# Layer 2's projections given out in denser steps and layer 1's in wider ones, in a list of sixteen interleaved graphs

## The chip, the cores and the metric

The kernel runs on one core of one Trainium2 chip. Its time is the device time of one execution in microseconds, the median over several executions. All executions told of here are in the fast state, so that no difference below mixes states. "The profile" is one execution taken by the hardware profiler. Its engines are PE (TensorE matrix products), PEld (TensorE weight loads), DVE (VectorE), ACT (ScalarE), POOL (GpSimd) and SP (SyncE); a q behind an engine's name marks its queue of issued transfers.

## The reference

Sixteen graphs of 1024 nodes with 256 features pass through four layers. Each layer normalizes, applies a ReLU, computes a graph layer and adds the result to its input.

```python
for layer in (L0, L1, L2, L3):
    h = jnp.maximum(_layernorm(x, axis=-1), 0.0)
    x = x + layer(h, adj)
# L0: h W, attention with a softmax over columns, elu
# L1: h W, attention with a softmax over rows, elu
# L2: relu(h W_upd + mean of the neighbours' h W_msg + bias)
# L3: attention with 4 heads of 64, relu, a norm of its own per head
```

All arithmetic is in float32. The sixteen graphs do not depend on each other.

## The kernel before

Each graph is a Python generator that emits instructions and yields a number: how many list units later its next piece is to stand. One loop merges all graphs into one list. Graph b starts at 120 b, and a graph's yields add up to some 260 units, so its second half stands beside the first half of the next graph.

```python
APART = 120.0
queue = [(33, 0, more())] + [(b * APART, b, graph(b)) for b in range(B)] + [(b * APART - 60, b, loads(b)) for b in range(1, B)]
while queue:
    queue.sort(key=lambda g: g[:2])
    at, b, g = queue.pop(0)
    ...
        queue.append((at + next(g), b, g))
```

A scheduler then makes a fixed order for each engine out of this list; it may move instructions past others, except where `later` keeps instructions in program order. At run time each engine works through its order; in the traces below an engine stands before an instruction that waits although other work is listed behind it.

```python
def graph(b):
    ...
    for g in range(NT // 2):                 # NT = 8
        norm.pair(xs, g)                     # L623: statistics of x on DVE
        m.step()
        yield 2
    for layer, inputs in ((layer0, (m,)), (layer1, (m.bytes,)), (layer2, ())):
        yield 2
        ...
        yield from layer(b, xs, *inputs, norm, after)
    yield 2
    ...                                      # layer 3, then the tail (L929 to L946)
```

Layer 0 has eight projections, then a row that goes to memory and comes back on all partitions, then eight weight tiles on DVE. Two output tiles are accumulated while the weights are made, the "early pairs":

```python
def layer0(b, xs, m, norm, after):
    for n in range(NT):
        ps = project(norm, wx[0], n, D + 2)          # L659 on PE; PSUM pool of 2 buffers
        nc.scalar.activation(hs[:, n, : D + 2], ...) # L717
        m.step()
        yield 1.2
    row_a, row_b = [everywhere(d, "row") for d in spread(column(...), 1, (1.0, S), "l0")]
    ...            # spread: PE L672 transposes the column, SP L678 writes it; everywhere: SP L684 reads the row
    yield 5
    for j in range(NT):
        nc.vector.scalar_tensor_tensor(p, row_a, q[:, j : j + 1], row_b, ...)        # L740
        nc.vector.scalar_tensor_tensor(p, p, 1.0, mask[:, j, :], ...)                # L742
        nc.scalar.activation(hs[:, j, :D], hs[:, j, :D], AF.Copy, scale=z[:, 1:2])   # L744
        ...        # early pair j - 1: PE L730, held in program order by later
        yield 2.6
    ...            # the eighth early pair, then six more output tiles, yield 3.9 each
```

The two loops that change, and what follows them:

```python
def layer1(b, xs, mask, norm, after):
    for n in range(NT):
        ps = project(norm, wx[1], n, D + 2)
        nc.scalar.activation(hs[:, n, : D + 2], ps[:, : D + 2], AF.Copy, scale=norm.rs[n])   # L773
        yield 1.2
    ...
    yield 5
    ...            # eight weight tiles on DVE (L793), yield 1.3 each; eight outputs on PE (L786), 3.9 each

def layer2(b, xs, norm, after):
    ...
    for n in range(NT):
        ps = project(norm, wx[2], n, 2 * D)
        nc.scalar.activation(hi[:, n, :D], ps[:, :D], ...)      # L832
        nc.scalar.activation(rest, ps[:, :D], ...)              # L834
        nc.scalar.activation(up[:, n, :D], ps[:, D:], ...)      # L835
        nc.vector.tensor_tensor(lo[:, n, :D], ...)              # L836
        nc.vector.tensor_tensor(up[:, n, :D], ...)              # L837
        yield 1.9
    for j in range(NT):
        ...        # one message tile: 16 products (PE L844) on the adjacency (POOL L585), ACT L853 empties it
        yield 3.5
```

Layer 3 waits 8 units after its projections, then makes 4 heads of 8 weight tiles (DVE L887, PE L893). The tail is DVE work of 128x1024 (L941 to L945) and ends with the output stores on SyncE (L946). The input of graph b is loaded by GpSimd (L545) into one of three buffers, so this load waits for the last L945 of graph b - 3, which read that buffer.

Of the kernel before, what the change touches and what calls it, by code (L numbers as in the profile page):

```python
# [421 lines left out]
def tile_simple_stack(  # L422
# [233 lines left out]
    def project(norm, w, n, width):  # L656
        ps = mm_ps.tile([P, HALF], F32, tag="mm", name="ps_proj")
        for c in range(DC):
            nc.tensor.matmul(ps[:, :width], norm.ht[:, c, n * P : (n + 1) * P], w[:, c, :width], start=(c == 0), stop=(c == DC - 1))  # L659
        return ps  # L660

    def new_hs(name="hs"):
        return state.tile([P, NT, W3], F32, tag="hs", name=name, bufs=4)

    def spread(col, n, scales, name):




        k = n * NT  # L670
        ps = tr_ps.tile([P, P], F32, tag="tr", name="ps_col")
        nc.tensor.transpose(ps[:k, :], col, ident)  # L672
        all_rows = []
        for scale in scales:
            e = small.tile([H * NT, P], F32, tag="e_row", name="e_row", bufs=2)
            nc.scalar.activation(e[:k, :], ps[:k, :], AF.Exp, scale=scale)
            d = dram.tile([n, N], F32, tag=f"row_{name}", name="d_row", bufs=4)
            later(nc.sync.dma_start(d.rearrange("r (t p) -> (r t) p", p=P), e[:k, :]))  # L678
            all_rows += [d[r] for r in range(n)]
        return all_rows  # L680
# [6 lines left out]
    def column(src, n):  # L687

        col = small.tile([P, H, NT], F32, tag="col", name="col", bufs=2)
        nc.vector.tensor_copy(col[:, :n, :], src.rearrange("p t n -> p n t"))  # L690
        return col[:, :n, :].rearrange("p n t -> p (n t)")
# [5 lines left out]
    def weights(name):  # L697
        return work.tile([P, N], F32, tag="p", name=name, bufs=NT)
# [70 lines left out]
    def layer1(b, xs, mask, norm, after):  # L769
        hs = new_hs()  # L770
        for n in range(NT):
            ps = project(norm, wx[1], n, D + 2)
            nc.scalar.activation(hs[:, n, : D + 2], ps[:, : D + 2], AF.Copy, scale=norm.rs[n])  # L773
            yield 1.2
        (d_row,) = spread(column(hs[:, :, D + 1 : D + 2], 1), 1, (S - 1.0,), "l1")
        row = everywhere(d_row, "row")
        watch(b, 1, hs[:, :, D : D + 2])
        q = small.tile([P, NT], F32, tag="q", name="q")
        nc.scalar.activation(q, hs[:, :, D], AF.Exp, scale=1.0 - S)
        nc.scalar.activation(hs[:, :, D], hs[:, :, D], AF.Exp, scale=S)  # L780
        yield 5
        ps_ = []
        early = [at_ps.tile([P, HALF], F32, tag="at", name="ps_o1") for _ in range(EARLY)]

        def product(ps, i, j):
            nc.tensor.matmul(  # L786
                ps[:, : D + 1], ps_[j][:, i * P : (i + 1) * P], hs[:, j, : D + 1], start=(j == 0), stop=(j == NT - 1)
            )

        for j in range(NT):  # L790
            nc.scalar.activation(hs[:, j, :D], hs[:, j, :D], AF.Copy, scale=hs[:, j, D : D + 1])
            p = weights("p1")
            nc.vector.scalar_tensor_tensor(p, row, q[:, j : j + 1], mask[:, j, :], op0=OP.max, op1=OP.mult)  # L793
            ps_.append(p)
            for i, ps in enumerate(early):
                product(ps, i, j)
            yield 1.3
        for i in range(NT):
            if i < EARLY:
                ps = early[i]  # L800
            else:
                ps = at_ps.tile([P, HALF], F32, tag="at", name="ps_o1")
                for j in range(NT):
                    product(ps, i, j)
            k = b * NT + i
            z = shares[:, k : k + 1]
            nc.vector.reciprocal(z, ps[:, D : D + 1])  # L807
            e = work.tile([P, D], F32, tag="e", name="e")
            nc.scalar.activation(e, ps[:, :D], AF.Exp, scale=z)  # L809
            v = work.tile([P, D], F32, tag="v", name="v")  # L810
            nc.scalar.activation(v, ps[:, :D], AF.Copy, scale=z)
            residual(xs, i, v, after, e)
            yield 3.9


    def layer2(b, xs, norm, after):
# [12 lines left out]
        for n in range(NT):  # L829
            ps = project(norm, wx[2], n, 2 * D)  # L830
            rs = norm.rs[n]
            nc.scalar.activation(hi[:, n, :D], ps[:, :D], AF.Copy, scale=rs)  # L832
            rest = work.tile([P, D], F32, tag="e", name="rest")
            nc.scalar.activation(rest, ps[:, :D], AF.Copy, scale=rs)  # L834
            nc.scalar.activation(up[:, n, :D], ps[:, D:], AF.Copy, scale=rs)  # L835
            nc.vector.tensor_tensor(lo[:, n, :D], rest, hi[:, n, :D].bitcast(F32), op=OP.subtract)  # L836
            nc.vector.tensor_tensor(up[:, n, :D], up[:, n, :D], rows["bias2"], op=OP.add)  # L837
            yield 1.9
        for j in range(NT):
            g, jj = divmod(j * P, QUART)  # L840
            ps = hd_ps.tile([P, HALF], F32, tag="hd", name="ps_o2")
# [240 lines left out]
```

## Time and profile before

| | |
|---|---|
| time | 2778.73 us (2765.97 to 2779.11) |
| span of the profiled execution | 2770.2 us |
| from the column transpose (L672) of layer 0 in one graph to that in the next, mean of graphs 3 to 14 | 166.8 us |
| start to the transpose of graph 1; transpose of graph 15 to the end | 158.5 us; 278.9 us |

The prediction shows the lines that bound the kernel. In a line of the page, behind the first bar stand the busy time and the mean ns of one instruction, behind the second the idle time ahead of the group and what ended most of it. Three lines of the view of waits are needed later: the waiting engine, tile and line, what it waited for, then microseconds in total, times, and the longest.

```profile
PE ps_o L730 <- ACT hs L744: 50.0, 29, 13.3
...
PE ps_proj L659 <- ACT up L835: 6.9, 17, 2.1
...
PE ps_o L786 <- DVE p L793: 3.7, 10, 0.4
```

Only the first is large: it is layer 0's early pairs, standing at the head of PE's order and waiting for the weights.

### The profile page before, as it was taken

How to read it: one execution, taken by the hardware profiler on the slowest of the kernel's cores; microseconds unless marked ns; L12 is line 12 of the kernel's file. 1: busy time of each engine (PE TensorE's matmuls, PEld its weight loads, DVE VectorE, ACT ScalarE, POOL GpSimd, SP SyncE). 2: the span in 40 equal slices, each digit the busy share in tenths (PEclk: the TensorE clock that was granted, in tenths of full speed). 3: DMA queues.
4: the chain of work that ended last, by engine and by line, in shares of the span. 5: the costliest groups of instructions: out<-in, count | busy, mean ns of one | idle time of the engine just before them, and what ended most of it. 6: DMA issues, size and time to landing. Idle time of an engine off the chain costs nothing.

```text
span 2770.2 us, 62256 instructions
## 1 busy us (share of the span) xinstructions
PE 2540.6 (92%) x25682; PEld 2014.7 (73%) x25682; DVE 2024.4 (73%) x4069; ACT 1440.6 (52%) x4065; POOL 371.8 (13%) x390
## 2 busy tenths in 40 slices
PE   5899999999999999999999999999999999999975
PEld 4677777777777767777776777767787677777754
DVE  4357768687676877768787676977768787676868
ACT  4563654627466373654627466373654637555250
POOL 1000110202011020210202111011210202111011
PEclk8899999999999999999999999999999999999997
DMA  4421322414124142322414124142332414223121
GB/s 150 105 77 55 110 72 68 114 52 137 51 74 118 60 118 67 97 76 78 115 52 137 52 78 114 59 119 66 96 77 78 115 51 126 62 66 95 40 62 34
DMA packets 146071, 233.71 MB, mean 84 GB/s; under 512 B 9392, under 2 KB 94512, under 8 KB 145776
## 3 DMA queue, kind: packets, MB, share of 16 engines
q1 hardware_dynamic: 74608, 145.73, 16.7%
q0 software_dynamic: 71168, 83.89, 12.0%
q8 instruction: 204, 3.34, 0.5%
q14 instruction: 91, 0.75, 0.1%
HBM read 212.35 MB, written 17.24 MB: 83 GB/s over the span
## 4 chain that ended last, share of the span: by engine, by line
PE 39%; DVE 22%; ACT 20%; issue 9%; DMA 7%; POOL 2%; SPq 0%; DVEq 0%; ACTq 0%; POOLq 0%
PE ps_o L893 11%; PE ps_o L730 9%; PE ps_proj L659 7%; PE ps_o L786 6%; DVE p L887 6%; ACT hn L631 5%; ACT unread L635 4%; DVE p L793 4%; DMA adj<-in_adj 3%; PE ps_o L844 3%; ACT mask L575 3%; DMA raw<-in_adj_t 2%; ACT ht L654 2%; PE pt_h L653 2%; DVE xs L708 1%
## 5 line engine op out<-in xcount | busy, mean ns | idle before, releaser
L887 DVE SCALAR_TENSOR_TENSOR p<-row,q,mask 128x1024 f32<-128x1024 f32 x512 | 636.8, 1280 | 62.3 <-DMA row<-d_row 41.3
L659 PE MATMUL ps_proj<-wx,ht 128*128 128x258 f32 (+2 forms) x2048 | 628.0, 444 | 21.4 <-ACT hs L717 9.9
L893 PEld LDWEIGHTS ps_o<-hb,p 128*64 128x64 f32 x16384 | 515.7, 138 | 157.3 <-issue 95.1
L893 PE MATMUL ps_o<-hb,p 128*64 128x65 f32 x16384 | 569.9, 225 | 43.1 <-DVE p L887 22.0
L730 PE MATMUL ps_o<-hs,p 128*128 128x256 f32 x2048 | 500.4, 388 | 56.1 <-ACT hs L744 50.0
L786 PE MATMUL ps_o<-hs,p 128*128 128x257 f32 x2048 | 526.8, 394 | 16.1 <-ACT mask L575 7.3
L659 PEld LDWEIGHTS ps_proj<-wx,ht 128*128 128x128 f32 x2048 | 364.8, 190 | 202.9 <-issue 72.3
L730 PEld LDWEIGHTS ps_o<-hs,p 128*128 128x128 f32 x2048 | 381.0, 193 | 118.2 <-ACT hs L744 59.8
L786 PEld LDWEIGHTS ps_o<-hs,p 128*128 128x128 f32 x2048 | 364.6, 190 | 79.6 <-issue 25.4
L707 DVE SCALAR_TENSOR_TENSOR xs<-e,xs 128x256 f32<-128x256 f32 x256 | 108.8, 425 | 323.5 <-ACT e L762 245.7
L631 ACT ACTIVATE hn<-xs,shift 128x256 f32<-128x256 f32 x512 | 237.5, 505 | 172.6 <-DVE shift L627 165.1
L809 ACT ACTIVATE e<-ps_o,shares 128x256 f32<-128x256 f32 x128 | 60.2, 470 | 422.1 <-DVE shares L807 422.0
L592 POOL TENSOR_SCALAR rs<-mv 128x4 f32<-128x4 f32 (+1 forms) x112 | 29.7, 265 | 1704.6 <-ACT unread L635 1694.1
L593 POOL TENSOR_TENSOR rs<-rs,neg_half 128x4 f32<-128x4 f32 (+2 forms) x144 | 238.3, 1665 | 8.2
L844 PE MATMUL ps_o<-hi,adj 128*128 128x258 f32 x1024 | 184.4, 313 | 25.3 <-DMA adj<-in_adj 15.6
L575 ACT ACTIVATE mask<-raw 128x512 uint8<-128x512 int32 x256 | 160.3, 630 | 66.1 <-DMA raw<-in_adj_t 65.3
L635 ACT ACTIVATE unread<-xs,shift 128x256 bf16<-128x256 f32 x384 | 193.1, 503 | 1.6
L653 PE MATMUL pt_h<-ident,hn 128*128 128x128 f32 x1024 | 174.2, 284 | 19.4 <-ACT hn L631 19.1
L654 ACT COPY ht<-pt_h 128x512 f32<-128x512 f32 x256 | 147.4, 588 | 72.2 <-PE pt_h L653 72.2
L653 PEld LDWEIGHTS pt_h<-ident,hn 128*128 128x128 f32 x1024 | 118.0, 142 | 84.6 <-ACT hn L631 63.3
L708 DVE SCALAR_TENSOR_TENSOR xs<-v,xs 128x256 f32<-128x256 f32 x384 | 161.8, 424 | 22.0 <-ACT v L764 3.5
L844 PEld LDWEIGHTS ps_o<-hi,adj 128*128 128x128 f32 x1024 | 143.5, 195 | 45.3 <-issue 15.8
(101 smaller groups left out, 2693.1 us busy)
## 6 DMA issues: line engine op xcount, KB each, us to landing
raw<-in_adj_t SPq DMA_DIRECT2D x256, 256.0 KB
adj<-in_adj POOLq DMA_DIRECT2D x64, 1024.0 KB, 5.9
row<-d_row SPq DMA_DIRECT2D x112, 512.0 KB
xs<-in_x POOLq DMA_DIRECT2D x32, 512.0 KB, 7.0
out<-res SPq DMA_DIRECT2D x32, 512.0 KB
wx<-in_w SPq DMA_DIRECT2D x3, 256.0 KB
d_row<-e_row SPq DMA_DIRECT2D x48, 4.0 KB
wts<-in_w_t SPq DMA_DIRECT2D x2, 256.0 KB
```

Of the source, the lines that this page charges most:

```text
L575: nc.scalar.activation(self.bytes[:, n, g * HALF : (g + 1) * HALF], raw, AF.Square, accum_out=squares[:, k : k + 1])
L593: nc.gpsimd.tensor_tensor(rs[:, :n], rs[:, :n], neg_half[:, :n], op=OP.pow)
L631: nc.scalar.activation(hn, xs[:, 2 * g + k, :], AF.Relu, bias=shift[:, k : k + 1])
L635: nc.scalar.activation(unread, xs[:, 2 * g + k, :], AF.Square, bias=shift[:, k : k + 1], accum_out=self.var[:, 2 * g + k : 2 * g + k + 1])
L653: nc.tensor.transpose(pt[:, c, k * P : (k + 1) * P], hn[:, c * P : (c + 1) * P], ident)
L654: nc.scalar.copy(self.ht[:, :, g * 2 * P : (g + 1) * 2 * P], pt)
L659: nc.tensor.matmul(ps[:, :width], norm.ht[:, c, n * P : (n + 1) * P], w[:, c, :width], start=(c == 0), stop=(c == DC - 1))
L730: m = nc.tensor.matmul(ps[:, :D], ps_[j][:, i * P : (i + 1) * P], hs[:, j, :D], start=(j == 0), stop=(j == NT - 1))
L786: nc.tensor.matmul(ps[:, : D + 1], ps_[j][:, i * P : (i + 1) * P], hs[:, j, : D + 1], start=(j == 0), stop=(j == NT - 1))
L844: nc.tensor.matmul(ps[:, : D + 2], adj_n[g][:, i, jj : jj + P], h[:, i, : D + 2], start=(h is hi and i == 0), stop=(h is lo and i == NT - 1),)
L887: nc.vector.scalar_tensor_tensor(p, row, q[:, j, h : h + 1], mask[:, j, :], op0=OP.max, op1=OP.mult)
L893: nc.tensor.matmul(pss[g][part, k * HW : (k + 1) * HW], p[:, i * P : (i + 1) * P][:, part], hbv[:, j, h, :], start=(j == 0 and k == 0), st ...
```

## The change

The intent is to move layer 2 against the next graph's layer 0. No instruction is added or removed, and two numbers change:

```diff
@@ layer1, behind each of its eight projections
-            yield 1.2
+            yield 1.4
@@ layer2, behind each of its eight projections
-            yield 1.9
+            yield 1.1
```

The places follow by adding up the yields. With the graph's start as 0, the next graph's layer 0 projects from 130.0 to 138.4 and makes weights from 144.6 on; its eighth early pair is listed at 165.4. Layer 2's first projection moves from 136.8 to 138.4, its first message from 152.0 to 147.2, layer 3's first projection from 182.0 to 177.2.

> **What bounds the kernel now.** I read the page first, then four windows that make one period of the steady state, then the order of work inside the first of them.
>
> ```profile
> span 2770.2 us, 62256 instructions
> PE 2540.6 (92%) x25682; PEld 2014.7 (73%) x25682; DVE 2024.4 (73%) x4069; ACT 1440.6 (52%) x4065; POOL 371.8 (13%) x390
> ...
> PE   5899999999999999999999999999999999999975
> ...
> PEclk8899999999999999999999999999999999999997
> ```
>
> The TensorE is the bound nearly everywhere. Only the first slice and the last two are thin, and neither end holds the two lines that change beside another graph for long. The clock is full after the first 140 us, so no clock effect is at stake. Sixteen graphs pass through, each starting 120 list units after the one before. From the first VectorE instruction of layer 0's weights (L740) of graph 6 (999.3) to that of graph 7 (1165.8) it is 166.5 us, and this repeats within a microsecond for all graphs from the third on. One such period, cut at the last layer-0 projection product of graph 6 (990.3), at its last early product (1027.0), at graph 5's first and last layer-3 product, and at the same projection point of graph 7:
>
> ```profile
> 990.30:1027.00 36.70, 31.74 (x165) 23.84 (x163) 34.03 (x71) 19.65 (x55) 5.80 (x8) 1.00 0.69 180
> 1027.00:1067.30 40.30, 39.54 (x201) 32.59 (x201) 17.88 (x54) 27.19 (x84) 6.42 (x8) 1.00 0.21 54
> 1067.30:1130.30 63.00, 60.51 (x1131) 49.55 (x1131) 56.52 (x92) 18.54 (x50) 3.83 (x5) 1.00 0.15 48
> 1130.30:1156.80 26.50, 25.15 (x111) 18.16 (x111) 17.53 (x38) 23.91 (x66) 7.00 (x6) 1.00 0.30 100
> ```
>
> The columns are PE, PEld, DVE, ACT and POOL busy. The first window is the one with most open PE time, 5.0 of 36.7 us, and there DVE is busy for 34.0: layer 0's weights make the pace. In that window layer 2 of graph 5 (projections, then messages) runs beside layer 0 of graph 6. Its end shows the mechanism:
>
> ```profile
> 1021.70 1.03 PE L730 MATMUL ps_o<-hs,p 128*128 128x256 f32 x4
> 1022.57 1.50 PE L659 MATMUL ps_proj<-wx,ht 128*128 128x264 f32 x6
> 1023.90 1.03 PE L730 MATMUL ps_o<-hs,p 128*128 128x256 f32 x4
> 1024.77 0.60 PE L653 MATMUL pt_h<-ident,hn 128*128 128x128 f32 x4
> 1026.94 1.13 PE L730 MATMUL ps_o<-hs,p 128*128 128x256 f32 x4 [1.57 <-ACT hs L744]
> ```
>
> PE stands still before the eighth early pair of layer 0, although two of layer 2's eight message tiles are still to do; they stand behind it in PE's order. Over the whole run that wait is one of the largest of PE:
>
> ```profile
> L730 PE MATMUL ps_o<-hs,p 128*128 128x256 f32 x2048 | 500.4, 388 | 56.1 <-ACT hs L744 50.0
> ```
>
> **What the Trainium skill says.** "Perfetto Trace Analysis", section Optimization Strategy, says that where the most contended engine changes over time, interleaving the regimes may help: this change moves such an interleaving. "TensorE: Matmul & The Clock Gate", section "Architectural detail", says that ACT and DVE queues are strictly in order and that TensorE can only pull weight loads ahead. The lines above agree: four transposes end at 1025.4 and nothing passes the pair that waits. Perfetto Trace Analysis, section Identifying the Most-Contended Engine, warns that matmul busy time is no measure of the distance to the limit. The trace agrees: if each matmul is given only the median step from one end to the next of its kind (0.436 us for a 258-column projection of two records, 0.858 for a 512-column one, 0.432 for layer 0's product, 0.434 for layer 1's, 0.120 for a message product, 0.067 for a layer-3 product, 0.110 for a transpose), a graph needs 147.3 us, so 19 of the 166.5 are lost, though PE shows 157 busy.
>
> **The change part by part.** No instruction is added or removed; both programs have the same counts. Only the list positions move: layer 2's eight projections take 8 x 1.1 = 8.8 units in place of 15.2, layer 1's 8 x 1.4 = 11.2 in place of 9.6. So layer 2's messages come 4.8 units earlier against the next graph, and layer 3 and the tail too. The scheduler turns list order into a fixed order per engine; I built the changed kernel and read that order for middle graphs, pricing PE rows with the steps above and DVE rows likewise (1.18 to 1.22 us for the 128x1024 ones, 0.34 to 0.43 for the 128x256 ones).
>
> Window 1, layer 0's column transpose to the eighth early pair. Before, the order has 30.4 us of PE work ahead of that pair and it took 36.5, a loss of 6.1. In the changed order all eight message tiles stand ahead of it: 33.0 us of work (34.1 for the later graphs). The chain that the pair waits for is hardly longer: DVE from the first L740 to the last L742 has 24.6 us before, 25.0 after. It may start a little sooner. Before, five tail operations of 1.14 us (L941 to L945) and ten small ones lie between the column copy and L740, 9.4 us; after, none or two of the five. But the row itself came only about 8.5 us after the copy in the transfer records, so at most 1 us is gained. In the later graphs (ninth on) an output store now stands ahead of the row's transfers in the same queue, waiting for a tail operation that ends about 3.2 us after the copy, when the row's data are ready at 2.1; I take up to 2 us off for them. So the window takes about 36 to 37 us again but with 2.6 to 3.7 us more work done: the loss falls from 6.1 to about 3.
>
> Window 2, to the first layer-3 product: 37.9 us of work becomes 31.9; the loss of 2.4 has other causes (the last norm before layer 3) and I keep it.
>
> Window 3, layer 3's heads beside layer 1: PE work 55.8 to 54.0, DVE 56.4 to 53.4. It took 63.0, so 7.2 is lost, part of it to changes between 64-column and 128-column products; those go from 23 runs of layer-3 products to 22. I take 6.9.
>
> Window 4, to the next column transpose: 23.2 us of work becomes 28.4 (27.3 for the later graphs), the loss of 3.3 stays; ACT is the busy one here (23.9 of 26.5), and the layer-1 outputs keep their 3.9 units.
>
> Losses: 3.0 + 2.4 + 6.9 + 3.3 = 15.6 in place of 6.1 + 2.4 + 7.2 + 3.3 = 19.0. That is 3.4 us per period, and with 14 such periods 48 us, to about 2731. The start (graph 0 alone, low clock) and the end (graph 15 alone in layers 2 and 3, the last 120 us) keep their time: with no neighbour the list distances do not matter. I trust the count for its sign more than its size: filling one in-order wait usually uncovers the next a microsecond later. I take off a third and predict 2747 us.
>
> **The rivals.**
> First, the freed time turns into a new wait in the same window, and nothing is gained. Message tile k needs the PSUM buffer of tile k-2 evacuated by ACT, and ACT is in order too: before, a message product waited 2.29 us at 1015.2 for such an evacuation behind L744. The fifth tile needs the third quarter of the adjacency, whose load is issued only after the second tile and lands 5.9 us later; 15.6 us of PE's idle time in the run has that cause. In the changed order 32 message products and four layer-0 products lie between, 5.6 us, against 4.7 before, so the distance does not shrink. For this rival: DVE's 25 us chain is untouched and PE's 33 us is now close to it, so any slip shows. Against: more work stands ahead of the wait than before, whatever slips. It gives 2765 to 2785.
>
> Second, the change is larger: the earlier tail takes DVE work away from layer 3's heads (3.0 us of 56.4) and from the start of layer 0, and if DVE rather than the mixture sets window 3, its time falls by 3 rather than 2, and window 1 starts 1 us sooner. That makes 5 to 6 us per period, about 2700. Against: window 3's DVE is busy 56.5 of 63.0, so it is not the only bound.
>
> Third, layer 1's row comes late. In the changed SyncE order the third head's row load stands ahead of layer 1's transfers, and its buffer is free only when the first head's eight weights are done. If layer 1's column is ready earlier than that, layer 1's products come late and window 3 runs on layer 3's products alone, paced by DVE at 1.2 us for each weight tile, whose sixteen products cost PE 1.07. That could cost 1 to 3 us per period, giving 2780 to 2800. Against: in PE's new order 176 layer-3 products precede layer 1's column transpose, more than the first head's 128, so the load should be free by then.
>
> **Range and chances.** The main count gives 2731, the first and third rival no gain or a small loss, the second about 2700. Predicted 2747 us, 2708 to 2788 eight times in ten. Two per cent faster means below 2723, which needs more than 55 us, above my full count: 0.18. Two per cent slower would be 2834, 4 us more loss per period, which only the third rival approaches: 0.04. Within 2%: 0.78.
>
> **What would show it.** The period should be near 164 us between first L740s of consecutive graphs. The eighth early pair should wait less than 1 us, and the last message product should come before it; the waits of layer-0 products for L744 should fall below 35 us in total. Layer 3's stretch should be near 61 us, and the one behind it grow to 31 or so. PE's busy time should stay within 1% or so, the span shrinking through idle time and stretched matmuls. I am wrong if the period stays at 166 or more: then waits on evacuations (L853), on the adjacency, or on layer 1's row will have grown, and the list of waits names which. A changed clock in the middle of the run, or a lengthened end after graph 14 is done, would be a cause that I have not priced.

## The result, and the profile after

The changed kernel takes 2706.78 us (2703.32 to 2710.86, four runs), beside 2778.92 us for the kernel before in the same rounds (four runs). A ratio here is the mean time of one kernel's fast runs over that of the other's of the same rounds, so not quite the ratio of the medians. It is 0.975, with a 95% interval from 0.9719 to 0.9781: 2.5% faster. Both kernels' outputs are right. The predicted time was 40 us too long, the measured one lies 1 us below the predicted range of 2708 to 2788, and "within 2%" was wrong.

First the page of the changed kernel:

```profile
span 2701.4 us, 62281 instructions
...
PE 2504.5 (93%) x25682; PEld 2018.0 (75%) x25682; DVE 2021.2 (75%) x4069; ACT 1432.5 (53%) x4065; POOL 418.1 (15%) x390
...
PE   5899999999999999999999999999999999999985
...
PEclk7899999999999999999999999999999999999998
```

The counts of PE, DVE and ACT are those of before and their busy times nearly so (PE 1.4% less); the clock row differs by a tenth in the first and the last slice. The span is 68.8 us shorter than the 2770.2 us of before. In the view of waits, L730 lost most of its wait, and L786 and L844 gained one:

```profile
PE ps_o L786 <- DVE p L793: 41.0, 15, 4.5
PE ps_o L844 <- ACT hi L832: 23.7, 14, 3.1
...
PE ps_o L730 <- ACT hs L744: 14.0, 2, 13.0
...
PE ps_proj L659 <- ACT up L835: 5.6, 13, 1.0
```

Of the 14.0 us left, 13.0 are a single wait at the start of the run. In the middle of the run, the eighth early pair now passes without one. Here is PE at that pair of graph 10 (start, duration, work):

```profile
1660.99 0.61 PE L659 MATMUL ps_proj<-wx,ht 128*128 128x264 f32 x2
1661.43 1.03 PE L730 MATMUL ps_o<-hs,p 128*128 128x256 f32 x4
1662.29 1.05 PE L659 MATMUL ps_proj<-wx,ht 128*128 128x264 f32 x4
1663.18 1.03 PE L730 MATMUL ps_o<-hs,p 128*128 128x256 f32 x4
```

The L730 lines carry no bracket of idle time, where the matching line of before had 1.57 us. The last message product has ended by 1661.1, and layer 3's projections (264 columns wide) fill the gaps between the pairs.

The period of graph 10, cut at the corresponding events of the prediction's four windows (PE, PEld, DVE, ACT and POOL busy, clock, DMA share, GB/s):

```profile
1625.30:1663.20 37.90, 35.78 (x197) 27.36 (x196) 31.40 (x75) 23.60 (x68) 5.83 (x8) 1.00 0.63 177
1663.20:1695.40 32.20, 32.20 (x160) 27.33 (x158) 15.15 (x44) 22.05 (x70) 3.11 (x5) 1.00 0.25 66
1695.40:1755.50 60.10, 57.48 (x1121) 47.57 (x1121) 55.27 (x84) 17.15 (x47) 3.18 (x2) 1.00 0.17 55
1755.50:1785.60 30.10, 28.88 (x132) 21.84 (x133) 23.65 (x51) 26.98 (x73) 14.16 (x10) 1.00 0.26 77
```

The first stretch holds 197 PE instructions where it held 165, in about the same time, and the second is 8 us shorter and has no open PE time left.

Single graphs differ a little, so the table below takes means over graphs 3 to 14. "Work" is the PE instructions in the stretch times the steps of each kind that the prediction lists, and "loss" is elapsed time less work. The loss is the quantity that a new order can change; the work only moves between stretches.

| stretch | before: elapsed, work, loss | after: elapsed, work, loss |
|---|---|---|
| 1: column transpose to eighth early pair | 36.3, 30.4, 5.9 | 38.4, 33.6, 4.8 |
| 2: to the first layer-3 product | 40.9, 37.9, 3.0 | 32.5, 31.9, 0.6 |
| 3: to the last layer-3 product | 62.8, 55.8, 7.0 | 61.0, 54.0, 7.0 |
| 4: to the next column transpose | 26.8, 23.2, 3.6 | 31.3, 27.9, 3.4 |
| period | 166.8, loss 19.5 | 163.1, loss 15.8 |

Over the whole run, the transpose of graph 1 comes 4.5 us earlier (154.0 for 158.5), the stretch from there to the transpose of graph 15 takes 2279.6 us in place of 2332.8, 53.2 less or 3.8 for each of 14 periods, and from there to the end it is 267.8 in place of 278.9, 11.0 less. Together that is the whole difference. Each number is from one execution. How far executions differ can be seen from e5_last_only and e14_end below, whose lists are those of before almost up to graph 15's transpose: 156.8 and 155.8 us for the first part, 2342.3 and 2341.6 for the second. So the 4.5 us at the start are not clear of this spread; the other two differences are.

One thing in stretch 1 became worse. Its weights start later: the first L740 comes 11.9 us after the column transpose, before it was 9.2. The transfers show what stands in the way. Before, in graph 6, the column is written (L678), its two rows are read (L684), and only after that does GpSimd issue the input of a later graph (L545). Lines of three engines, in order of time:

```profile
991.80 0.64 SPq L678 DMA_DIRECT2D d_row<-e_row  x2
993.03 0.82 SPq L684 DMA_DIRECT2D row<-d_row  x2
...
998.64 1.59 POOL L545 DMA_DIRECT2D xs<-in_x  x2 [7.13 <-DVE res L945]
...
999.26 2.48 DVE L740 SCALAR_TENSOR_TENSOR p<-row,q 128x1024 f32<-128x1024 f32 x2
```

After, in graph 10:

```profile
1626.83 1.59 POOL L545 DMA_DIRECT2D xs<-in_x  x2 [4.20 <-DVE res L945]
...
1627.01 0.91 SPq L678 DMA_DIRECT2D d_row<-e_row  x2
1629.78 2.78 SPq L684 DMA_DIRECT2D row<-d_row  x2
...
1637.32 1.28 DVE L740 SCALAR_TENSOR_TENSOR p<-row,q 128x1024 f32<-128x1024 f32 x1 [0.81 <-DMA row<-d_row]
```

In both, the load waits for L945, the tail's last step, which frees its buffer. The tail stands earlier in the changed list, so the megabyte of input now goes out 3.0 us ahead of the row's read where it went out 5.6 us behind it. That was a suspicion at this point; the last experiments test it.

### The profile page after: what moved, and what is told of

Same layout as the page of the kernel before. It is cut to its first block, busy times and chain, and to the rows that moved or that the text cites. A ratio compares the mean times of both kernels' runs of the same rounds, so it can differ in the third digit from the quotient of the medians.

```text
span 2701.4 us, 62281 instructions
## 1 busy us (share of the span) xinstructions
PE 2504.5 (93%) x25682; PEld 2018.0 (75%) x25682; DVE 2021.2 (75%) x4069; ACT 1432.5 (53%) x4065; POOL 418.1 (15%) x390
## 4 chain that ended last, share of the span: by engine, by line
PE 50%; DMA 13%; issue 13%; DVE 13%; ACT 10%; POOL 1%; SPq 0%; DVEq 0%; POOLq 0%; ACTq 0%
PE ps_o L893 14%; PE ps_o L730 12%; PE ps_proj L659 9%; PE ps_o L786 9%; DMA raw<-in_adj_t 5%; PE ps_o L844 5%; DVE p L887 4%; DMA adj<-in_adj 4%; DMA row<-d_row 3%; PE pt_h L653 2%; ACT hn L631 2%; ACT mask L575 2%; ACT unread L635 1%; DMA d_row<-e_row 1%; DVE p L793 1%
## 5 line engine op out<-in xcount | busy, mean ns | idle before, releaser
L659 PE MATMUL ps_proj<-wx,ht 128*128 128x258 f32 (+2 forms) x2048 | 631.5, 444 | 19.4 <-ACT hs L717 12.8
L893 PE MATMUL ps_o<-hb,p 128*64 128x65 f32 x16384 | 563.1, 225 | 16.2 <-DVE p L887 11.1
L786 PE MATMUL ps_o<-hs,p 128*128 128x257 f32 x2048 | 529.7, 398 | 50.0 <-DVE p L793 41.0
L730 PE MATMUL ps_o<-hs,p 128*128 128x256 f32 x2048 | 492.6, 387 | 14.5 <-ACT hs L744 14.0
L786 PEld LDWEIGHTS ps_o<-hs,p 128*128 128x128 f32 x2048 | 372.1, 193 | 112.6 <-issue 48.5
L730 PEld LDWEIGHTS ps_o<-hs,p 128*128 128x128 f32 x2048 | 383.8, 193 | 70.7 <-ACT hs L744 15.3
L592 POOL TENSOR_SCALAR rs<-mv 128x4 f32<-128x4 f32 (+1 forms) x112 | 56.9, 508 | 1600.3 <-ACT unread L635 1584.7
L593 POOL TENSOR_TENSOR rs<-rs,neg_half 128x4 f32<-128x4 f32 (+2 forms) x144 | 259.7, 1806 | 10.7
L575 ACT ACTIVATE mask<-raw 128x512 uint8<-128x512 int32 x256 | 160.5, 630 | 133.8 <-DMA raw<-in_adj_t 114.7
L844 PE MATMUL ps_o<-hi,adj 128*128 128x258 f32 x1024 | 184.9, 308 | 35.5 <-ACT hi L832 23.7
L844 PEld LDWEIGHTS ps_o<-hi,adj 128*128 128x128 f32 x1024 | 144.3, 192 | 60.7 <-ACT hi L832 29.7
L740 DVE SCALAR_TENSOR_TENSOR p<-row,q 128x1024 f32<-128x1024 f32 x128 | 161.1, 1269 | 30.5 <-DMA row<-d_row 30.5
L654 ACT COPY ht<-pt_h 128x512 f32<-128x512 f32 x256 | 147.2, 588 | 67.3 <-PE pt_h L653 66.8
```

Of the source, the lines that this page charges most:

```text
L575: nc.scalar.activation(self.bytes[:, n, g * HALF : (g + 1) * HALF], raw, AF.Square, accum_out=squares[:, k : k + 1])
L593: nc.gpsimd.tensor_tensor(rs[:, :n], rs[:, :n], neg_half[:, :n], op=OP.pow)
L659: nc.tensor.matmul(ps[:, :width], norm.ht[:, c, n * P : (n + 1) * P], w[:, c, :width], start=(c == 0), stop=(c == DC - 1))
L730: m = nc.tensor.matmul(ps[:, :D], ps_[j][:, i * P : (i + 1) * P], hs[:, j, :D], start=(j == 0), stop=(j == NT - 1))
L786: nc.tensor.matmul(ps[:, : D + 1], ps_[j][:, i * P : (i + 1) * P], hs[:, j, : D + 1], start=(j == 0), stop=(j == NT - 1))
L844: nc.tensor.matmul(ps[:, : D + 2], adj_n[g][:, i, jj : jj + P], h[:, i, : D + 2], start=(h is hi and i == 0), stop=(h is lo and i == NT - 1),)
```

## The experiments

All experiments are timed beside the kernel before on the same chip, all gave right results, and all compared runs are fast. The last three (e21_x_late to e23_before_x_late) ran on another chip than the rest, so ratios are compared and not times. The theories, with the letters that the expectations use (where an expectation spells a theory out, its own words count):

- A: the place of layer 2's messages ahead of layer 0's in-order wait is what gains. Layer 1's number then matters little by itself. A2 is A with layer 1's part counted as a place too: its 1.6 units set everything behind it back.
- B: the packing of layer 2's projections gains by itself.
- C: the wider spacing of layer 1's projections gains by itself, because it eases the work beside them.
- D: layer 3 and the tail standing earlier gains.

### Layer 2 alone (e1_l2_dense)

```diff
@@ layer2
-            yield 1.9
+            yield 1.1
```

> Only layer 2's projections in denser steps (1.1), layer 1's as before (1.2); messages, layer 3 and tail now 6.4 list units earlier. Theory A (earlier messages, layer 3 and tail against the next graph are what pays): as good as the whole change or a little better, 2690 to 2715 us. Theory B (the packing of the projections itself pays): the same, 2700 to 2715. Theory C (layer 1's wider steps relieve layer 3's heads): most of the gain missing, 2740 or more.

Measured: 2758.89 us, ratio 0.9935 (0.9910 to 0.9961). The waits of this run:

```profile
PE ps_o L786 <- DVE p L793: 47.3, 16, 7.3
PE ps_proj L659 <- ACT up L835: 44.8, 49, 4.5
...
PE ps_o L730 <- ACT hs L744: 14.0, 2, 13.0
```

The in-order wait for L744 is gone exactly as in the full change, and yet only a quarter of the gain is there. In its place PE waits 44.8 us, some three times per graph, for L835: a dense projection finds both PSUM buffers of the projections full. The list suggests a collision, because layer 2 projects from 136.8 and layer 0 of the next graph until 138.4 with the same two buffers. The traces speak against it. 38.3 of the 44.8 us come behind the column transpose, when layer 0 has done its last projection, and e3_dense_pause below, with the same places and steps of these projections, has 7.5 us of this wait and none behind the transpose. What e3_dense_pause does not have is the earlier tail, which lets the next input go (L545). In graph 10 of e1_l2_dense, whose transpose is at 1648.66:

```profile
1645.54 1.59 POOL L545 DMA_DIRECT2D xs<-in_x  x2 [2.50 <-DVE res L945]
...
1654.39 0.63 ACT L575 ACTIVATE mask<-raw 128x512 uint8<-128x512 int32 x1 [3.95 <-DMA raw<-in_adj_t]
...
1656.26 4.13 PE L659 MATMUL ps_proj<-wx,ht 128*128 128x512 f32 x9 [3.77 <-ACT up L835]
```

ACT, which empties the projections, stands 3.95 us for a tile of the adjacency mask, and DVE stands 4.94 us at L623 for the input; so PE stands for ACT. This is read from the trace: e1_l2_dense was not run with the load held back. Theory A's number was missed: the wait left PE's list and the time did not.

### Layer 1 alone (e2_l1_wide)

```diff
@@ layer1
-            yield 1.2
+            yield 1.4
```

> Only layer 1's projections in wider steps (1.4), layer 2's as before (1.9); everything after layer 1's projections 1.6 units later. Theory A: no gain, rather a small loss, 2775 to 2800 us. Theory B: as before, 2770 to 2785. Theory C: most of the gain, 2710 to 2745.

Measured: 2746.53 us, ratio 0.9889 (0.9863 to 0.9915). The part that theory A holds for minor gains more than the other. Its wait for L744 fell by half, although layer 2's messages stand 1.6 units later than before:

```profile
PE ps_o L730 <- ACT hs L744: 23.5, 17, 13.0
```

### Packing without a new place (e3_dense_pause)

```diff
@@ layer2
-            yield 1.9
+            yield 1.1
+        yield 6.4          # behind the eight projections: the messages start where they did
```

> Layer 2's projections at 1.1, but a pause of 6.4 units after them, so that messages, layer 3 and tail stand in the list where they stood before. Theory A: the gain is gone, 2760 to 2785 us. Theory B: the gain stays, 2700 to 2720. Theory C: as before, 2770 to 2785.

Measured: 2785.05 us, ratio 1.0035 (1.0023 to 1.0047). Packing alone, with messages and tail in their old places, costs a little. B falls.

### Layer 3's heads and the tail earlier, nothing else (e4_l3_early)

```diff
@@ layer3, behind its projections
-        yield 8
+        yield 3.2
```

> Layers 1 and 2 as before; the list pause ahead of layer 3's heads 3.2 units in place of 8, so that heads and tail come 4.8 earlier and the messages stay. PE work ahead of layer 0's eighth early pair stays 30.4 us. Theory A in two parts, about half from the messages: 2735 to 2755 us. Rival D (heads and tail alone carry it): 2700 to 2720. If the messages alone carry it: 2765 to 2785.

Measured: 2769.28 us, ratio 0.9974 (0.9960 to 0.9989). A tenth of the gain. D falls as the main cause, with a reservation: the earlier tail lets the input go earlier here too. The first L740 comes 13.9 us after the column transpose in place of 9.2, and the loss of stretch 1 is 7.8 us in place of 5.9. What D is worth without this was not tested.

### Layer 1's delay without its spacing (e9_delay)

```diff
@@ layer1, behind its projections (which keep 1.2)
-        yield 5
+        yield 6.6
@@ layer2
-            yield 1.9
+            yield 1.1
```

> Layer 2 dense (1.1); layer 1's projections at the old 1.2, and the 1.6 units given back as a longer list pause after them (6.6 in place of 5), so that layer 1's weights and all later stages stand in the list as in the full change. Theory A2 (layer 1's wider steps help only by setting the later stages 1.6 units back, so that layer 2's projections miss layer 0's projections of the next graph): as the full change, 2695 to 2720 us. Theory C (the spacing of layer 1's projections among layer 3's heads is worth something by itself): as layer 2 alone, 2745 to 2765.

Measured: 2712.19 us, ratio 0.9771 (0.9753 to 0.9789). Nearly the whole gain. What layer 1's number does beside layer 2's is to set layer 2 back by 1.6 units.

### Layer 1's spacing without its delay (e10_width)

```diff
@@ layer1, behind each projection, and behind all eight
-            yield 1.2
+            yield 1.4
-        yield 5
+        yield 3.4
@@ layer2
-            yield 1.9
+            yield 1.1
```

> Layer 2 dense (1.1), layer 1's projections wide (1.4), but the pause after them shortened by 1.6 (3.4 in place of 5), so that later stages stand as with layer 2 alone. Theory A2: as layer 2 alone, 2745 to 2770 us. Theory C: as the full change, 2695 to 2720.

Measured: 2740.21 us, ratio 0.9868 (0.9845 to 0.9891). Layer 2 stands as in e1_l2_dense, and the wait for L835 is there again, 44.9 us in all. This is still 0.7% better than that run, so C is right in a small part: at this place the spacing itself is worth something. The view of waits shows where: L786 waits 10.9 us for L793, and 47.3 in e1_l2_dense. Why the spacing does this was not tested.

### The tail's new place with late messages (e8_l2_shift)

```diff
@@ layer1
-            yield 1.2
+            yield 1.4
@@ layer2, behind each message tile (the projections keep 1.9)
-            yield 3.5
+            yield 2.7
```

> Layer 1 wide (1.4), layer 2's projections at the old 1.9, its message tiles at 2.7 in place of 3.5: layer 3 and the tail come exactly where the full change puts them, layer 2's projections are not packed and its messages start 6.4 later. Theory A2 (where layer 3 and the tail stand is what counts for their three quarters of the period): most of the gain in the steady state, 2710 to 2735 us. Theory B (packed projections are needed): 2740 to 2765.

Measured: 2745.29 us, ratio 0.9895 (0.9875 to 0.9915). Layer 3 and the tail stand as in the full change, the messages do not, and the time is that of layer 1 alone. So the tail's new place adds nothing to layer 1's number alone as long as the messages are late. The reservation of e4_l3_early holds here too: the first L740 comes 13.0 us after the transpose, in e2_l1_wide 9.0.

### Layer 2's place by another way (e11_combined)

```diff
@@ layer1, behind its projections (each 1.4)
-        yield 5
+        yield 3.4
@@ graph, ahead of a layer
-            yield 2
+            yield 3.6 if layer is layer2 else 2
```

These edits are on the changed kernel. Layer 1's outputs stand earlier, layer 2 where the change has it.

> Meant to beat the full change: layer 1's projections wide (1.4) but the pause after them shortened by 1.6, so its weights keep their old place; layer 2 dense, and the 1.6 given back just ahead of layer 2, so that layer 2 and all after it stand as in the full change. The changed kernel loses 2.8 us per period where layer 1's products wait for their weights, the same without the 1.6 units lost 0.6. If that wait is free to save: 2670 to 2695 us. If the loss only moves elsewhere: 2700 to 2720.

Measured: 2712.60 us, ratio 0.9750 (0.9719 to 0.9780): no better and no worse than the change. Waits of L786 for L793 are 48.8 us here, so this does not remove them.

### Farther the same way (e15_wider)

```diff
@@ layer1 (changed kernel)
-            yield 1.4
+            yield 1.6
```

> Dose: layer 1 at 1.6, layer 2 at 1.1, so layer 2's projections come 3.2 units later than with layer 2 alone, its messages 3.2 earlier than before in place of 4.8. If layer 2's projections only had to be moved off the next graph's layer-0 projections, more delay does no harm: 2695 to 2715 us. If message tiles ahead of layer 0's waits and room for the projections are traded against each other, the full change is near the best: 2715 to 2740.

Measured: 2758.54 us, ratio 0.9913 (0.9887 to 0.9939). Two thirds of the gain are lost, and the first wait is back while the other is small:

```profile
PE ps_o L730 <- ACT hs L744: 49.3, 20, 13.1
...
PE ps_proj L659 <- ACT up L835: 7.7, 17, 1.0
```

So the gain has an edge on either side: the pair that waits for L744 on the late side, and on the early side ACT and DVE, which stand for transfers beside the early load. The list places of these runs, sorted by layer 2's first message, show it (next graph: projections until 138.4, weights from 144.6):

| kernel | layer 2's first projection | first message | layer 3's first projection | ratio |
|---|---|---|---|---|
| e1_l2_dense | 136.8 | 145.6 | 175.6 | 0.9935 |
| e10_width | 136.8 | 145.6 | 175.6 | 0.9868 |
| after | 138.4 | 147.2 | 177.2 | 0.9750 |
| e9_delay | 138.4 | 147.2 | 177.2 | 0.9771 |
| e11_combined | 138.4 | 147.2 | 177.2 | 0.9750 |
| e15_wider | 140.0 | 148.8 | 178.8 | 0.9913 |
| before | 136.8 | 152.0 | 182.0 | 1 |
| e3_dense_pause | 136.8 | 152.0 | 182.0 | 1.0035 |
| e2_l1_wide | 138.4 | 153.6 | 183.6 | 0.9889 |
| e8_l2_shift | 138.4 | 153.6 | 177.2 | 0.9895 |

A step of 1.6 units to either side of the change costs from half to three quarters of the gain. The three kernels with the same places have the same time to about 0.2%, however they got there. The last two rows keep the wider projections of before, so they are not one series with the others.

### The two ends: the last graph, the first two, the last but one

All three take the numbers of the change for some graphs and those of before for the others.

```diff
@@ layer1, layer2   (e5_last_only)
+            yield 1.4 if b == B - 1 else 1.2
+            yield 1.1 if b == B - 1 else 1.9
@@ layer1, layer2   (e13_start)
+            yield 1.4 if b < 2 else 1.2
+            yield 1.1 if b < 2 else 1.9
@@ layer1, layer2   (e14_end)
+            yield 1.4 if b == B - 2 else 1.2
+            yield 1.1 if b == B - 2 else 1.9
```

> The whole change for the last graph alone. The full change gained 11 us between the last graph's layer-0 column transpose and the end, which the prediction had put at nothing, and layer 2 alone gained 9 there. If that comes from the last graph's own list: 10 us less than before, 2762 to 2770 us. If it comes from the graph ahead of it (its layer 3 and tail are then out of the way): no gain, 2772 to 2782.

> The whole change for graphs 0 and 1 alone. In the full change the column transpose of graph 3's layer 0 came 14 us earlier. If the start's gain is their own and additive: 2760 to 2770 us (8 to 14 less). If it needs the following graphs changed: 2772 to 2782.

> The whole change for graph 14 alone, the one ahead of the last. The change for the last graph alone gave nothing, so the 11 us at the end should come from here: 2762 to 2770 us. If they need both graphs: 2772 to 2782.

Measured: e5_last_only 2777.53 us, ratio 1.0003 (0.9982 to 1.0023); e13_start 2771.07 us, ratio 0.9964 (0.9943 to 0.9986); e14_end 2767.68 us, ratio 0.9958 (0.9935 to 0.9981).

Changing graph 15, the one without a neighbour behind it, gives nothing. The gain after the last transpose therefore comes from the graph ahead: graph 14's layers 2 and 3 and its tail stand beside graph 15's layers 0 and 1 there. In the trace of the changed kernel, counted from the transpose of graph 15, graph 14's layer-3 products end at 129.9 us in place of 140.4, and graph 15's own stages then follow about 11 us earlier to the end. In e14_end they end at 130.1, in e5_last_only at 138.4. What follows differs by some 6 us between executions even with the numbers of before in both last graphs (138.5 us in before, 144.0 in e13_start), so the end is better read from the times than from one trace. The first two graphs alone give 0.4% as well; in the trace the transpose of graph 3 comes at 476.1 us, as in the full change (476.2; before 490.0).

### The late row: the output store (e17_out_pool), DVE's order (e19_stats_late), both (e20_stats_out)

Three suspects for the late L740 in stretch 1: the output store that stands ahead of the row in SyncE's queue (the prediction's suspect), the statistics of the next input (L623) that DVE has ahead of L740 and that wait for the input, and the input load itself on the DMA engines. These runs edit the changed kernel.

```diff
@@ tail (e17_out_pool, e20_stats_out)
-            later(nc.sync.dma_start(out[...], of))
+            later(nc.gpsimd.dma_start(out[...], of))
@@ Norm.pair (e19_stats_late, e20_stats_out): kept behind L740
-                    nc.vector.bn_stats(st, xs[:, k, :])
+                    later(nc.vector.bn_stats(st, xs[:, k, :]))
@@ layer0 (e19_stats_late, e20_stats_out)
-            nc.vector.scalar_tensor_tensor(p, row_a, q[:, j : j + 1], row_b, ...)
+            later(nc.vector.scalar_tensor_tensor(p, row_a, q[:, j : j + 1], row_b, ...))
```

> The changed kernel with the output stores issued by GpSimd, so that they no longer stand ahead of layer 0's row transfers in SyncE's queue. In the changed kernel L740 starts 12 us after the column transpose, 9.3 before the change. If the store is what holds the row: L740 starts 2 to 3 us sooner in graphs 9 to 15 and the time is 2670 to 2690 us. If VectorE, which stands before L740 in bn_stats of the next graph waiting for its x load, is ready only then anyway: 2695 to 2715.

> The changed kernel with the next graph's bn_stats kept behind layer 0's first weight step (L740) in VectorE's order; output stores as they were. VectorE no longer stands 3.5 us waiting for the x load, but the row still lands behind the output store. If the row alone sets L740's start: 2695 to 2712 us. If VectorE's wait for x sets it: 2670 to 2690.

> Both: output stores by GpSimd and bn_stats behind L740. If the two waits stand side by side ahead of L740 and hide each other, only this run gains: L740 starts about 3 us sooner, the period falls by 2 to 3 us, 2660 to 2685 us. If the loss of the first window has another cause: 2695 to 2715.

Measured: e17_out_pool 2748.64 us, ratio 0.9896 (0.9860 to 0.9932); e19_stats_late 2728.01 us, ratio 0.9817 (0.9786 to 0.9848); e20_stats_out 2759.08 us, ratio 0.9934 (0.9912 to 0.9956). All are slower than the change. L740 comes 12.0, 12.7 and 12.2 us after the transpose, no earlier than its 11.9. So neither edit brought the row earlier. In e17_out_pool the store did leave one part of the way and burden another: in graphs 9 to 14 the time from the column's write to the row's read falls from 2.8 to 1.2 us, but from the read to L740 it grows from 7.4 to 10.1. Why this kernel is slower by 42 us with L740 no later is not settled: its wait of L844 for L832 is 36.9 us, in the change 23.7, and PE's order moved as well, as it did in e19_stats_late, so these are not clean tests. "DMA: Bandwidth & Descriptors" of the Trainium skill, section "Issuing engines are not separate DMA queues", says that transfers started by different engines run on the same 16 DMA engines and interleave. e17_out_pool agrees: with the store in another queue the way from write to L740 took 11.3 us in these graphs, in the change 10.2.

### The input load later (e21_x_late), and with the store moved (e22_x_late_out)

The load of the input is made to wait for data: a small copy from the previous graph's first weight tile of layer 0 into the load's buffer must come first. The kernel has this device already for the first graphs (`behind` copies from the last entry of `gates`).

```diff
@@ load_x (both, on the changed kernel)
-        if 0 < b < 3:
+        if 0 < b:
@@ layer0
-            if b == 0:
+            if b == 0 or (b > 1 and j == 0):
                 gates.append(p)
@@ tail (e22_x_late_out only)
-            later(nc.sync.dma_start(out[...], of))
+            later(nc.gpsimd.dma_start(out[...], of))
```

> The changed kernel with the next graph's x load held until layer 0's weights of the graph before are done (from graph 3 on); TensorE's order stays that of the changed kernel. In it the x load is let go earlier than before the change, by the earlier tail, and its 1 MB then moves beside the row that layer 0's weights wait for (296 GB/s against 168 at that point). If that contention is what makes the row land 7.5 us after its issue in place of 5.3: L740 starts 2 to 4 us sooner after the column transpose, the first window takes 35 to 36 us, 2665 to 2690 us. If the row is late for another reason: 2700 to 2715.

> The same, with the output stores issued by GpSimd besides. If the store ahead of the row's transfers in SyncE's queue costs something of its own once the x load is out of the way: another 1 us per period, 2650 to 2675 us. If only the bytes count, wherever they are issued: as e21, or worse by as much as the stores alone were (about 40 us).

Measured: e21_x_late **2678.42 us**, ratio 0.9654 (0.9613 to 0.9694); e22_x_late_out 2685.98 us, ratio 0.9685 (0.9644 to 0.9726). The first is the fastest kernel of the study. Its interval lies wholly below that of the change, and 0.9654 / 0.975 = 0.990: one per cent better than the change. PE's order is that of the change. In the trace, L545 now comes 31 to 34 us behind the row's read, and L740 9.5 us after the transpose:

```profile
1612.23 0.82 SPq L684 DMA_DIRECT2D row<-d_row  x2
...
1617.91 1.28 DVE L740 SCALAR_TENSOR_TENSOR p<-row,q 128x1024 f32<-128x1024 f32 x1
...
1642.84 0.81 POOL L545 DMA_DIRECT2D xs<-in_x  x1
```

The load comes later than the hold alone asks, because GpSimd's order now has four loads of the adjacency ahead of it; DVE's wait for the input at L623 is 30.9 us in all, in the change 49.2. The wait of L844 for L832, 23.7 us in the change, is gone, while those of L786 for L793 (40.3) and of L730 for L744 (13.8) stay. Stretch 1 takes 35.5 us with a loss of 1.9, the period 160.8.

PE's wait that went is not one for the row itself. Here is graph 10 of the changed kernel again, with the mask tile that SyncE issues (L566) only behind the row, 7.4 us after the transpose:

```profile
1637.87 0.63 ACT L575 ACTIVATE mask<-raw 128x512 uint8<-128x512 int32 x1 [1.82 <-DMA raw<-in_adj_t]
...
1639.00 0.39 PE L844 MATMUL ps_o<-hi,adj 128*128 128x258 f32 x1 [1.37 <-ACT hi L832]
```

L832, which the first message needs, stands behind this L575 in ACT's order, and DVE stands 3.48 us at L623 for the input. In e21_x_late L566 is issued 5.4 us after the transpose, L575 waits 0.25 us, and L623 is not in this stretch. So the hold takes away three delays at once: of the row, of the mask tile behind it in SyncE's queue, and of DVE. That the load causes the loss is shown; what each of the three is worth was not tested.

Where the 2.7 us of the row went can now be cut in three: from the transpose to the column's write, to the row's read, to L740 (means of graphs 3 to 14; the middle one also for graphs 3 to 8 and 9 to 14):

| kernel | transpose to write | write to read (3 to 8; 9 to 14) | read to L740 | sum |
|---|---|---|---|---|
| before | 1.6 | 1.2 (1.2; 1.2) | 6.5 | 9.2 |
| after | 1.6 | 3.7 (4.6; 2.8) | 6.6 | 11.9 |
| e21_x_late | 1.7 | 2.0 (1.4; 2.7) | 5.8 | 9.5 |

With the load held, 1.7 us less pass between write and read and 0.8 less behind the read. In the later graphs, where the output store stands ahead, 1.5 us more than before remain between write and read. e22_x_late_out tests these: with the store moved they are gone (1.2 us), L740 comes 9.3 to 9.6 us after the transpose in place of 10.1, and the kernel is still no faster. So the prediction's suspect is real for these graphs, but smaller, and not by its wait: the write itself is issued 1.8 us after the transpose, before 1.6.

Two more kernels, with a fourth buffer for the input in place of the hold, did not fit: the build reported 73 kb needed where 71.6 kb were left.

### The control: the same hold in the kernel before (e23_before_x_late)

```diff
@@ the edits of e21_x_late, with the numbers of before
-            yield 1.4
+            yield 1.2
-            yield 1.1
+            yield 1.9
```

> Control: the kernel before with the next graph's x load held in the same way. There the x load is let go by the tail's last operation only after the row has landed, so holding it longer should do nothing: 2765 to 2785 us. If it gains about 30 us here too, the x load was a burden of both kernels and not one that the change brought.

Measured: 2781.86 us, ratio 1.0026 (1.0007 to 1.0044). The hold gains nothing there, and the three parts of the row's way are those of before, to the tenth. In the kernel before the load costs nothing that shows in the time: the change itself put it in the way.

### The losses side by side

Means over graphs 3 to 14, computed as above; the last two columns are the loss of the period and the time from graph 15's transpose to the end:

| kernel | stretch 1 | stretch 2 | stretch 3 | stretch 4 | period | loss | end |
|---|---|---|---|---|---|---|---|
| before | 5.9 | 3.0 | 7.0 | 3.6 | 166.8 | 19.5 | 278.9 |
| e1_l2_dense | 6.6 | 1.3 | 7.9 | 3.6 | 166.7 | 19.4 | 269.5 |
| e2_l1_wide | 4.4 | 3.2 | 8.6 | 1.5 | 165.0 | 17.7 | 278.5 |
| after | 4.8 | 0.6 | 7.0 | 3.4 | 163.1 | 15.8 | 267.8 |
| e10_width | 6.9 | 1.5 | 6.9 | 3.6 | 166.1 | 18.8 | 266.7 |
| e15_wider | 7.8 | 1.1 | 7.2 | 3.3 | 166.8 | 19.5 | 275.1 |
| e21_x_late | 1.9 | 0.8 | 7.5 | 3.2 | 160.8 | 13.5 | 270.6 |

Each row is one execution, and periods of the kernel before differ by up to 0.7 us between executions. The gain at the end belongs to layer 2 (e1_l2_dense has it, e2_l1_wide does not), and e1_l2_dense gains nearly nothing in the steady state.

## Why the prediction was right or wrong

**The steady state: right, before the deduction.** The period of 164 us was 163.1, and the full count of 48 us for 14 periods was 53.2 in the trace. Its marks in the profile came true but for one (PE's busy time fell by 1.4%, not by 1% or so): waits for L744 14.0 us in all (below 35), the eighth pair after the last message product and without a wait, stretch 3 at 61.0, stretch 4 at 31.3.

**"I take off a third": the first step that failed.** The reason, that filling one in-order wait usually uncovers the next, was right in kind: the change added 37.3 us of waits of L786 for L793 and 23.7 of L844 for L832. But the count of 3.4 us per period, which has no such term, held in sum, 3.7 by the table of stretches. Stepping down from 48 to 32 us made 16 us of the 40.

**"The start … and the end … keep their time: with no neighbour the list distances do not matter": the second step that failed.** In the traces 4.5 us at the start and 11.0 at the end came out of these two parts, 15.6 us in all; the 11.0 are borne out by the time of e14_end (0.42% less), while the 4.5 are within the spread of executions. The end as the prediction drew it still has a neighbour: graph 14 runs beside graph 15's layers 0 and 1 for more than half of it, and e14_end shows that it is graph 14 that gives the gain, while e5_last_only, the part that truly has no neighbour, gives none. Whether the start gained anything before graph 1's transpose stays open. With the full count and the 11.0 of the end the prediction would have been 2778.7 - 48 - 11.0, about 2720 us.

**Stretch 1: sign right, size wrong.** The row "at most 1 us" sooner, "up to 2 us" later for the later graphs: the first L740 came 2.7 us later on average. The loss fell by 1.1 in place of 3. The cause named, the output store, is real in graphs 9 to 14 (1.5 us with the load out of the way). The larger one was missed: the tail frees the input's buffer earlier, and the input's load then meets the row and the mask tile behind it, and holds DVE at L623. e21_x_late takes it away and the loss is 1.9; e23_before_x_late shows that it was not there before.

**Stretch 2: "The loss of 2.4 has other causes … and I keep it": wrong, to the good.** It fell from 3.0 to 0.6. In graph 10 of the changed kernel the first layer-3 product comes after 10 instructions of layer 1's projections, in graph 6 of before after 20, and the stretch had no open PE time left. That this order is the reason was not tested. Stretch 2's 2.4 made up for stretch 1's missing 1.9: the period was right partly because two errors cancelled.

**Layer 1's part: a size that the prediction didn't give.** The count priced the two numbers as one order. The runs show that layer 2's number alone gives 0.65% and layer 1's alone 1.1%, while together they give 2.5%. Beside layer 2's number it is the delay of 1.6 units that counts (e9_delay): with it the waits for L835 are 5.6 us, without it 44.8. By the traces it does so by letting the tail, and the input's load, come later, and not by keeping the projections of layers 2 and 0 apart; that was not tested.

**The rivals.** The first came half true: new waits appeared, in layer 1 and at the first message rather than at the evacuations, and the one of L844 on the adjacency shrank from 15.6 to 11.6 us; it did not eat the gain. The second's total, about 2700 us, was near, but not by its way: stretch 3 kept its loss of 7.0 us and stretch 1 did not start sooner. The third, a late row of layer 1, hardly showed (DVE's waits of L793 for its row are 9.2 us, before 6.2).

**Two loose readings.** The period repeats within 1.5 us of 166.5, not within one (165.0 to 167.7 between first L740s), and the clock row is below full in the last slice too.

The new wait of L786 is left in place. DVE's order puts five weight tiles of layer 3 ahead of layer 1's first one, while PE's order has layer 1's products ahead. In graph 6 of the changed kernel:

```profile
1061.74 6.16 DVE L887 SCALAR_TENSOR_TENSOR p<-row,q,mask 128x1024 f32<-128x1024 f32 x5 [0.34 <-PE ps_o L893]
1067.82 2.48 DVE L793 SCALAR_TENSOR_TENSOR p<-row,q,mask 128x1024 f32<-128x1024 f32 x2
```

and on PE:

```profile
1069.25 2.30 PE L786 MATMUL ps_o<-hs,p 128*128 128x257 f32 x8 [2.53 <-DVE p L793]
```

Still open: whether another order on DVE would win these 2.7 us per graph (41.0 / 15), why layer 1's number alone shortens stretches 1 and 4, why its spacing alone is worth 0.7% at e10_width's place, and how much e1_l2_dense, e10_width, e4_l3_early and e8_l2_shift would gain with the load held. In all four the first L740 comes 13.0 to 13.9 us after the transpose, so they were timed with a burden that e21_x_late shows can be taken away, and the edge on the early side may lie elsewhere without it.

## What to carry to other kernels

In a program made of interleaved copies, a new step between pieces is a shift of everything behind it. Price it by what the shifted work then stands beside, on both sides, because there are waits at either edge of the gain, and a step of 1.6 units each way cost half of it or more here. Ask also which buffers come free earlier and which load starts then: an early load can stand in the way of smaller transfers that DVE and ACT, and behind them PE, wait for, and a hold behind some data of the right moment gave another per cent. And compare where a wait falls in time before naming its cause: the waits for L835 looked like a collision in the list, and the trace had most of them after the other side was done. Count the first and the last copies too: all but the very last one have a neighbour behind them.

## What the Trainium skill lacked or had wrong

- "DMA: Bandwidth & Descriptors", section "Issuing engines are not separate DMA queues", says that transfers interleave, but not what a small one pays for a large one beside it. Here, in graphs 3 to 8, the time from a small write to the read of its row grew from 1.2 to 4.6 us when a megabyte of input started 6 to 7 us ahead of that read, and went back to 1.4 when the input was held.
- "Perfetto Trace Analysis", section Optimization Strategy, advises interleaving where the most contended engine changes, and does not say that this moves buffer releases, and so the starts of loads. Here that cost one per cent (ratio 0.9750 against 0.9654 with the load held).
- None of the pages cited says how narrow the gain of such an interleaving can be: layer 2's first message at 145.6, 147.2 and 148.8 list units, with layer 2's dense steps in all three, gave ratios of 0.9935, 0.9750 and 0.9913.
